# A fused attention and local-attention kernel: first loads reordered and halved, seven warm-up matmuls for ten, and the last result block handled in two halves of its rows

## The chip, the cores and the metric

The kernel runs on one core of a Trainium2 chip. The metric is the device time in microseconds of one execution. A core has five engines with instruction streams of their own: PE (TensorE: matmuls, with PEld for its weight loads), DVE (VectorE), ACT (ScalarE), POOL (GpSimd) and SP (SyncE). Engines wait for each other, and for transfers, through semaphores. SP and ACT also issue transfers between memory and the core. Such an issue takes time in the issuing engine's own stream, and whatever stands behind it in that stream waits until it is done.

## What is computed

The input x has 4 images of 64 x 64 pixels and 256 channels, in float32. Two layers follow each other:

```
# layer 0, over all 4096 pixels of an image
q = x @ Wq + bq ; k = x @ Wk + bk ; v = x @ Wv + bv        # 32, 32, 256 channels
x = gamma * softmax(q k^T) v + x
# layer 1
perceived = depthwise 3x3 convolution of x, 3 outputs per channel, + b_perc
dx = W_up2 gelu(W_up1 perceived + b_up1) + b_up2
h = x + dx
out = h + local attention of h over each pixel's 3x3 window
```

## The kernel before

Channels lie on the 128 partitions, in two halves c = 0 and c = 1 (`CH` = 2). An image's pixels are cut into 8 blocks ("slots") of 512 pixels, that is 8 rows of 64; there are 32 slots in all. For each slot the main loop (line 1088) runs through 16 points. At each it forms energies (line 304), their exponentials (line 312) and the product with the values (line 323), while the convolution, the two-step update and the local attention of slots two to five places back are put in between. The order of the work on each engine is the order of the program's text (`manual_schedule`, line 1614).

**The start.** `renew(slot, cs)` (line 123) issues on SP's queue a load of one slot's rows of x into a ring tile `xp`; slots 0 and 1 come as one transfer for each channel half, slots 2 and 3 as one each. On ACT's queue go the weights `wqk` (line 129) and `wv` (line 131, through `loaded`, line 79), and then four small transfers that put the bias `bqk` on four groups of 32 partitions (line 138). While these run, PE executes `WARM` = 10 matmuls of a tile of ones with itself (line 152); a float32 matmul shows as two passes in the trace, so the trace has 20 of them. `fetch(0)` and `fetch(1)` (line 202) copy the arrived rows into dense tiles `xc`: half c = 0 by DVE (line 227), half c = 1 by ACT (line 229). ACT's first such instruction is preceded by an `ACT_TABLE_LOAD` that the compiler puts there; the trace shows it under line 229.

The first matmuls of the computation are those of `project_v(0, 0)` (line 263): for each of two groups of 128 pixels, the product with `wv[:, 0, :]` and then that with `wv[:, 1, :]`:

```
for i in range(2):
    for kin in range(CH):
        nc.tensor.matmul(ps[:, i * C : (i + 1) * C],
            lhsT=xc[:, kin, bass.ts(2 * pair + i, P)], rhs=wv[:, kin, :], ...)
```

So the second matmul needs half c = 1 of `xc` and of `wv`. Next come `project_qk(0)` (line 231; it needs `wqk` and both halves of slots 0 and 1) and the other products of `wv`. ACT drains these (lines 242 and 275), and SP and ACT send the keys and queries on to other partitions (lines 246, 254, 259) before the energies of slot 0 can begin.

**The end.** After the last slot of the main loop, the last blocks are finished one after another (lines 1219 to 1249). The last is slot 31: `local_product(last, 0)` (line 1259) and `local_product(last, 1, judge)` (line 1266), one for each channel half. Each is a group of matmuls (line 1025), a DVE multiplication with the reciprocal sums (line 1042), a DVE addition of the residual (line 1050) and a store on SP's queue (line 1051). `behind` is given only in the second of these two calls: `judge` (line 1261) sums a check of all values over the partitions and writes the flag `bad`. Every engine then reads that flag (`TENSOR_LOAD`, line 1616) and jumps over a second version of the whole computation (`COMPARE_BRANCH`, line 1616), which isn't executed here. Behind the jump the engines meet (line 1661), SP after it has waited for all transfers, and the program ends.

## Time and profile before

Four executions took 3455.48 to 3456.39 us, with a median of 3455.88 us.

| | |
|---|---|
| the profiled execution's own time | 3456.07 us |
| its span, from the first instruction to the last | 3454.2 us |
| granted TensorE clock over the span | 0.999 |
| instructions | 33708 |
| idle time of PE before the first matmul of the warm-up | 1.07 us |
| PE busy between 0 and 120 us | 117.2 us |
| last DVE instruction of the computation ends | 3449.47 us |

The transfers of the start, in the order of their issue on each queue:

| queue | what | issued at, us | KB | issue to landing, us |
|---|---|---|---|---|
| ACT | wqk | 0.8 | 64 | 3.2 |
| SP | x, slot 0, c = 0 | 0.8 | 264 | 3.0 |
| ACT | wv | 1.3 | 256 | 4.0 |
| SP | x, slot 0, c = 1 | 1.3 | 264 | 3.8 |
| SP | x, slot 1, c = 0 | 1.7 | 264 | 4.3 |
| ACT | bqk, first three | 1.7, 2.2, 2.7 | 0.1 | 4.5, 4.2, 4.0 |
| ACT | bqk, fourth | 3.9 | 0.1 | 3.0 |
| SP | x, slot 1, c = 1 | 4.0 | 264 | 3.0 |
| SP | x, slot 2 | 5.3 | 528 | 4.3 |
| SP | x, slot 3 | 6.0 | 528 | 4.9 |

And the two stores of the last slot, both on SP's queue: the first is issued at 3448.1 us and has landed 2.0 us later, the second is issued at 3449.5 us and has landed 2.9 us later; 256 KB each.

In lines of the profile, an engine's name with a q (SPq, ACTq) is its instruction stream: issues of transfers, waits, branches. In the chain of waits the columns are start, duration and what ran; in the rows of a timeline they are start, duration, engine, line, operation and count; in the view of one source line the numbers behind "x1:" are the shortest, median and longest duration in ns, and then the start of the first and last in us.

### The profile page before, as it was taken

The page shows a single profiled execution, that of the slowest core. Times are in us where ns is not written, and L with a number is a line of the kernel's source. Part 1 is how long each engine was busy: PE and PEld are TensorE (multiplying, and loading weights), DVE is VectorE, ACT ScalarE, POOL GpSimd, SP SyncE. Part 2 cuts the span into 40 slices and gives each one's busy share as a digit, 9 for nine tenths or more (in the row PEclk, how much of TensorE's full clock was granted, in tenths as well). Part 3 has the DMA queues.
Part 4 walks back from the last instruction along what each step waited for, and adds up shares of the span by engine and source line. Part 5 has one row for each costly group of instructions (what it writes and reads, how often), then busy time and mean ns, then how long its engine had stood idle before and what let it go on. Part 6 is the DMA issues. An engine that isn't in the chain of part 4 may idle for free.

```text
span 3454.2 us, 33708 instructions
## 1 busy us (share of the span) xinstructions
PE 3441.8 (100%) x12726; PEld 1999.5 (58%) x12726; DVE 2738.8 (79%) x4439; ACT 1064.0 (31%) x1328; POOL 359.5 (10%) x525
## 2 busy tenths in 40 slices
PE   9999999999999999999999999999999999999999
PEld 5445555556555556566555555566656555555555
DVE  2388888767888888876888888887688888888895
ACT  3232333323332233332333323333233333223331
POOL 2000001110111110111001111101110111110021
PEclk9999999999999999999999999999999999999999
DMA  3000000120000000012000000001100000000000
GB/s 107 7 4 10 7 10 16 28 47 18 16 13 10 16 16 16 22 25 46 16 10 16 10 13 16 16 22 30 42 16 16 16 10 7 16 16 18 7 7 26
DMA packets 93274, 67.05 MB, mean 19 GB/s; under 512 B 65872, under 2 KB 71248, under 8 KB 92976
## 3 DMA queue, kind: packets, MB, share of 16 engines
q1 hardware_dynamic: 92432, 64.42, 6.8%
q8 instruction: 102, 1.67, 0.2%
q14 instruction: 68, 0.56, 0.1%
q10 hardware_dynamic: 672, 0.39, 0.0%
HBM read 43.62 MB, written 18.81 MB: 18 GB/s over the span
## 4 chain that ended last, share of the span: by engine, by line
PE 98%; DVE 1%; SPq 0%; DMA 0%; ACT 0%; issue 0%; ACTq 0%; POOL 0%; DVEq 0%
PE acc L323 51%; PE e L304 8%; PE hid_gf L582 4%; PE hid_de L582 4%; PE hid_bc L582 4%; PE lv L891 3%; PE v L270 3%; PE lo L1025 3%; PE s L932 3%; PE hid_a L582 3%; PE dx_ab L534 2%; PE dx_eg L534 1%; PE dx_cd L534 1%; PE hid L614 1%; PE g_cd L534 1%; PE qk L236 1%
## 5 line engine op out<-in xcount | busy, mean ns | idle before, releaser
L323 PE MATMUL acc<-p,v 128*128 128x512 f32 x4096 | 1835.2, 594 | 0.3 <-DVE o L388 0.3
L323 PEld LDWEIGHTS acc<-p,v 128*128 128x128 f32 x4096 | 770.0, 190 | 808.0 <-issue 791.4
L477 DVE SCALAR_TENSOR_TENSOR perc<-xp,wperc,perc 128x512 f32<-128x512 f32 (+2 forms) x1554 | 1103.0, 772 | 27.5 <-ACT perc L473 27.4
L312 ACT ACTIVATE p<-e 128x1024 f32<-128x1024 f32 x512 | 524.0, 1024 | 1717.8 <-PE e L304 713.2
L337 DVE TENSOR_TENSOR den<-den,p 128x1024 f32<-128x1024 f32 x480 | 587.4, 1224 | 86.4 <-ACT p L312 84.7
L957 POOL TENSOR_TENSOR lp<-lp,near 128x396 f32<-128x396 f32 x60 | 97.0, 1617 | 2490.7 <-ACT lp L952 2490.7
L304 PE MATMUL e<-qa,ka 32*128 32x512 f32 x2048 | 292.1, 640 | 0.0
L304 PEld LDWEIGHTS e<-qa,ka 32*128 32x128 f32 x2048 | 80.1, 183 | 166.0 <-issue 145.1
L582 PE MATMUL hid_de<-perc,wmix 128*128 128x256 f32 x720 | 165.2, 379 | 0.0
L582 PEld LDWEIGHTS hid_de<-perc,wmix 128*128 128x128 f32 x720 | 137.1, 190 | 43.4 <-issue 21.5
L483 DVE TENSOR_TENSOR perc<-perc 128x256 f32<-128x256 f32 x360 | 153.6, 441 | 8.2
L605 ACT ACTIVATE hid<-hid,bup 128x512 f32<-128x512 f32 x120 | 80.1, 714 | 219.5 <-DVE hid L589 219.5
L473 ACT ACTIVATE perc<-xp,bperc,wperc 128x512 f32<-128x512 f32 x192 | 145.3, 805 | 1.8 <-DVE xp L394 1.8
L980 POOL TENSOR_TENSOR lsum<-lsum,lp 128x99 f32<-128x99 f32 x168 | 122.3, 734 | 11.0
L1025 PEld LDWEIGHTS lo<-lp,lv 128*128 128x128 f32 x732 | 102.9, 191 | 35.0 <-issue 27.2
L891 PE MATMUL lv<-wlv,h 128*128 128x256 f32 x520 | 122.4, 380 | 0.0
L589 DVE TENSOR_TENSOR hid<-hid_bc,hid 128x512 f32<-128x512 f32 x60 | 41.5, 692 | 101.7 <-PE hid_bc L582 101.7
L270 PE MATMUL v<-wv,xc 128*128 128x256 f32 x512 | 116.6, 380 | 0.1
L270 PEld LDWEIGHTS v<-wv,xc 128*128 128x128 f32 x512 | 97.1, 190 | 28.0 <-issue 14.8
L932 PEld LDWEIGHTS s<-lq,h 128*128 128x128 f32 x520 | 87.1, 188 | 37.3 <-issue 27.4
L891 PEld LDWEIGHTS lv<-wlv,h 128*128 128x128 f32 x520 | 99.0, 191 | 15.3 <-issue 2.1
L1025 PE MATMUL lo<-lp,lv 128*128 128x99 f32 (+1 forms) x732 | 107.5, 296 | 0.0
(194 smaller groups left out, 3108.6 us busy)
## 6 DMA issues: line engine op xcount, KB each, us to landing
xp<-in_x SPq DMA_DIRECT2D x30, 528.0 KB, 4.0
xc<-in_x SPq DMA_DIRECT2D x56, 256.0 KB, 3.6
out<-lo SPq DMA_DIRECT2D x56, 256.0 KB, 2.0
qa<-packed SPq DMA_DIRECT2D x124, 64.0 KB, 2.0
out<-res SPq DMA_DIRECT2D x8, 256.0 KB, 2.0
ka<-st SPq DMA_DIRECT2D x124, 16.0 KB, 1.8
packed<-st SPq DMA_DIRECT2D x31, 64.0 KB, 1.9
wup<-in_w_up SPq DMA_DIRECT2D x1, 1536.0 KB, 6.8
```

The costliest lines, as they stand in the source:

```text
L270: nc.tensor.matmul(ps[:, i * C : (i + 1) * C], lhsT=xc[:, kin, bass.ts(2 * pair + i, P)], rhs=wv[:, kin, :], start=(kin == 0), stop=(kin = ...
L304: nc.tensor.matmul(e[:, j, :], lhsT=key[rows, :], rhs=queries[s][rows, :], start=True, stop=True,)
L312: nc.scalar.activation(p, energies[s, G][:, 2 * half : 2 * half + 2, :], AF.Exp)
L323: nc.tensor.matmul(accs[s][c], lhsT=v[:, 2 * half + i, bass.ts(c, P)], rhs=p[:, i, :], start=(first and i == 0), stop=(G == NG - 1 and hal ...
L337: nc.vector.tensor_tensor(den, den, p, ALU.add)
L477: nc.vector.scalar_tensor_tensor(acc, win, wt, acc, ALU.mult, ALU.add)
L483: nc.vector.tensor_tensor(t[:, to, :], t[:, a, :], t[:, b, :], op)
L534: nc.tensor.matmul(ps[:, n * C : (n + 1) * C], lhsT=w(j), rhs=values(j), start=(j == 0), stop=(j == kin - 1),)
L582: nc.tensor.matmul(ps[:, n * C : (n + 1) * C], lhsT=w(j), rhs=mixes[s, j][:, kind, :], start=(j == 0), stop=(j == MULT - 1),)
L891: nc.tensor.matmul(ps[:, half * C : (half + 1) * C], lhsT=keys_of(s, t, half, kin), rhs=wlv[:, kin, :], start=(kin == 0), stop=(kin == CH ...
L932: nc.tensor.matmul(ps[:, t * QR * QW : t * QR * QW + rows * QW].rearrange("p (h w) -> p h w", w=QW), lhsT=keys_of(s, t, half, kin), rhs=gu ...
L1025: nc.tensor.matmul(pv[:, rows, columns(half)], lhsT=lvs[block, t, half][:, bass.ts(c, P)], rhs=near_ws[block, half][:, t, of, :], start=(i ...
```

## The change

`WARM` goes from 10 to 7. On ACT's queue `wv` comes first, as two transfers of one half each, and `wqk` after them; `wv` has the same tile as before, so `loaded` is no longer used for it. The loads on SP's queue keep their order. In `local_product`, the call that is given `behind`, which is that of slot 31 and c = 1 alone, does the residual and the store in two halves of four rows: each half has an addition of its own, and the first half's store goes out on SP's queue, the second's on ACT's. `KR` is 4 and n * C is n * 256 pixels, which is four rows.

```
-WARM = 10
+WARM = 7
...
         wqk = pool.tile([P, CH, 2, CQK], F32, tag="wqk", name="wqk")
+        wv = const.tile([P, CH, C], F32, tag="wv", name="wv")
+        nc.scalar.dma_start(out=wv[:, 0, :], in_=w_v[:, 0, :])
+        renew(0, slice(0, 1))
+        nc.scalar.dma_start(out=wv[:, 1, :], in_=w_v[:, 1, :])
+        renew(0, slice(1, 2))
         nc.scalar.dma_start(out=wqk, in_=w_qk)
-        renew(0, slice(0, 1))
-        wv = loaded(w_v, "wv", queue=nc.scalar)
-        renew(0, slice(1, 2))
         renew(1, slice(0, 1))
         renew(1, slice(1, 2))
...
             ov, rv = (t.rearrange("p (h a w) -> p h a w", a=2, w=KW) for t in (o, res))
-            nc.vector.tensor_tensor(rv, ov, pixels(s, c), ALU.add)
-            nc.sync.dma_start(out=out[b, :, c, bass.ts(g, NB)], in_=res)
+            if not behind:
+                nc.vector.tensor_tensor(rv, ov, pixels(s, c), ALU.add)
+                nc.sync.dma_start(out=out[b, :, c, bass.ts(g, NB)], in_=res)
+                return
+
+            for n, queue in enumerate((nc.sync, nc.scalar)):
+                rows = slice(n * KR, (n + 1) * KR)
+                nc.vector.tensor_tensor(rv[:, rows], ov[:, rows], pixels(s, c)[:, rows], ALU.add)
+                at = g * NB + n * C
+                queue.dma_start(out=out[b, :, c, at : at + C], in_=res[:, bass.ts(n, C)])
```

## The prediction

> **What bounds it now.** I read the page first: busy time of the engines and the chain of work that ended last.

> ```profile
> PE 3441.8 (100%) x12726; PEld 1999.5 (58%) x12726; DVE 2738.8 (79%) x4439; ACT 1064.0 (31%) x1328; POOL 359.5 (10%) x525
> ...
> PE 98%; DVE 1%; SPq 0%; DMA 0%; ACT 0%; issue 0%; ACTq 0%; POOL 0%; DVEq 0%
> ```

> PE is busy throughout, so what an edit away from PE can be worth lies before PE runs without gaps and behind its last matmul: some 6 us at the front and 7 us at the back. Both edits lie there. The second view is the chain of waits over the first 16 us:

> ```profile
> 0.82 3.03 DMA xp<-in_x
> 3.84 0.02 issue
> 3.86 0.32 ACTq L138
> 4.18 0.03 issue
> 4.21 1.28 ACT L229
> 5.49 0.01 issue
> 5.50 0.63 ACT xc L229
> 6.13 0.04 issue
> 6.18 1.56 PE v L270 x6
> ```

> The start hangs on ACT, not on the warm-up: the fourth bias transfer (L138) is issued only when the first half of x has landed at 3.84; behind it stand the table load and the copy of half c = 1, and PE's second product (the third of its eight passes) starts at 6.18. From that landing to PE it is 6.18 - 3.84 = 2.34 us. Why should a bias transfer wait for x? The waits of SP's queue tell, with the time of two landings (the transfers issued at 1.3 and 1.7):

> ```profile
> SPq L126 <- DMA wqk<-in_w_qk: 1.8, 1, 1.8
> SPq L126 <- DMA wv<-in_w_v: 1.0, 1, 1.0
> ```

> ```profile
> DMA to landing us min/median/max: 3.8/4.0/4.3
> ```

> Eight transfers go out without a wait: wqk, x0c0, wv, x0c1, bqk, x1c0, bqk, bqk. The ninth (x1c1) waits for wqk, the first; the tenth (fourth bqk) for x0c0, the second; the eleventh (x, slot 2) for wv, the third. So each transfer waits for the one eight places before it. x0c1, the fourth, lands at 1.27 + 3.8 = 5.06.

> Third, the row of the warm-up against later matmuls, in the timeline:

> ```profile
> 1.07 4.44 PE L152 MATMUL warm<-ones 128*128 128x128 f32 x20 [1.07 <-POOL ones L144]
> 9.54 5.45 PE L270 MATMUL v<-wv,xc 128*128 128x256 f32 x24
> ```

> A pass over 128 columns takes 4.44 / 20 = 0.22 us, later one over 256 columns 5.45 / 24 = 0.23: the array runs at half rate until about 5.2 us (the last of the warm-up's weight loads, at 5.1, is down from 334 to 244 ns), 4.1 us after its first pass.

> Last, the view of line 1616 for the end:

> ```profile
> L1616 ACTq COMPARE_BRANCH  x1: 54/54/54, 3448.7 to 3448.7; - x1
> ...
> L1616 DVEq COMPARE_BRANCH  x1: 72/72/72, 3449.7 to 3449.7; - x1
> ...
> L1616 SPq COMPARE_BRANCH  x1: 50/50/50, 3450.5 to 3450.5; - x1
> ...
> L1616 ACTq EVENT_SEMAPHORE  x1: 17/17/17, 3451.8 to 3451.8; - x1
> L1616 PEldq EVENT_SEMAPHORE  x1: 51/51/51, 3452.4 to 3452.4; - x1
> L1616 DVEq EVENT_SEMAPHORE  x1: 21/21/21, 3453.2 to 3453.2; - x1
> ```

> From branch to next instruction ACT needs 3.1 us and DVE 3.5. DVE, whose branch stands behind the last addition, comes last at 3453.2; the last store has landed at 3449.5 + 2.9 = 3452.4. So the end is set by a branch, not by the store, and the span closes 1.0 us behind it.

> **The change, part by part.** *Warm-up.* Three matmuls fewer are 6 passes of 0.213 us, 1.28 us of PE. The warm-up isn't in the chain: it ends at 5.5, the second product waits for ACT until 6.18. The two passes that can run earlier (about 4.4, when wv's first half and DVE's copy, 3.86 + 0.43, are there) hide in the same wait. Worth 0.

> *Order and halves of the loads.* wv in two halves makes thirteen transfers of twelve and seven issues on ACT of six. Before, the two queues took their places as A S A S A S A A S A S S; kept up, the new list is wv0, x0c0, wv1, x0c1, wqk, x1c0, bqk, bqk, x1c1, bqk, x slot 2, bqk, x slot 3. The third bqk is tenth and waits for x0c0 (about 3.9); the fourth is twelfth and waits for x0c1, the fourth: 5.06 instead of 3.84. Behind it on ACT stand the table load and the copy, and PE waits for these: 5.06 + 2.34 = 7.40 instead of 6.18, +1.22 us. Bounds: if no ACT issue had to wait, seven of 0.47 (0.81, 1.26, 1.74) would end at 4.1, the table load at 5.4, and PE would start at 6.07, -0.1. If the wait is for wv1 and this lands as late as the whole wv (1.3 + 4.0 = 5.3), +1.46. I take 1.22, since the places of the two queues are read from this trace. Transfers that move otherwise have cover: x1c1 now waits for wv0 (as wqk 3.2 to as wv 4.0 after 0.81, so 4.0 to 4.8), lands 3.0 later at 7.8 at most and is copied in 0.62, while its use, the second half of qk, moves to 7.40 + 1.56 + 0.93 = 9.9; without the shift it could cost 0.4. wqk, third on ACT at 1.74, lands by 6.2 at the first bqk's 4.5, ahead of qk at 9.0. The slot 2 load waits for wv1 instead of wv, no later than before.

> The shift goes on undiminished: behind 6.18 the chain is PE's v and qk, ACT's drains and issues, SP's issues, each started by the one before it; PE then is busy for good.

> *The clock.* Fourteen passes end at about 4.3, the two early products at half rate (0.43 each) at 5.3; then PE is idle until 7.40. If the full rate still comes at 5.2, this costs 0. If the 4.1 us start anew at 7.40, it comes at 11.5 and (11.5 - 7.4) / 2 = 2.05 us are lost. The four executions already differ by 0.9, about what a rate change moved by 1.8 us would do; I take half of that, 0.4, near the lower end since the array is all but gapless from 1.07 to 5.3.

> [...]

> *The end.* Additions over 128x256 take 0.42 each, two in a row 0.76 (L904), against 0.69 now (L1050): DVE's last is +0.07. SP's store goes out 0.3 us earlier, hidden since stores don't end last. ACT's own store is new: its stream now stands at the second half until 3449.54, issues, reads the flag and branches. SP did just that from 3449.5 and branched at 3450.5; so ACT at 3450.6 instead of 3448.7, and at its 3.1 us it is back at 3453.7, behind DVE's 3453.2: +0.5. Bounds: as quick as SP's own branch (SP goes on at 3450.7), and DVE decides: +0.1; PE's 3.6 (3448.8 to 3452.4): +1.0. I take ACT's own row. ACT's store lands by 3449.6 + 2.9 = 3452.5 and stays hidden.

> **Sum.** 1.22 + 0.4 + 0.5 = +2.1 us. The profiled execution took 3456.07 (span 3454.2, 1.9 around it): 3458.2. It lies 0.19 above the median 3455.88, so 3458.0 is the forecast. A difference under 0.2% (6.9 us) is about what a measurement of this kernel can't tell from no change; the forecast is +0.06%.

> **Rivals.** *The full rate comes late* (slower). Place: the matmuls from 7.40 on; price: half of the time from there to the full rate, on top of 1.7 us. At 11.5 it gives 3459.7, at 14 it gives 3460.9. It makes the kernel slower by more than 6.9 us from the point where the rate changes at 17.8 or later, which needs 10 us of half rate. For it: the gap from 5.3 to 7.4. Against: after 7.4 PE has work without such gaps, so a third try of 4.1 us is unlikely.

> *ACT isn't held* (the places of the queues differ, or the fourth bqk waits for x0c0): PE starts at 6.07 to 6.6, and the end alone remains: 3455.88 + 0.5 = 3456.4. For it: the places are inferred. Against: seven ACT transfers can't all be among the first eight unless SP's loads are held instead.

> *The halves pay* (faster): the first product's earlier start and a quicker last store show fully; at best -0.1 at the front, the clock always in time (the spread's half, -0.4), end 0: 3455.4. Against: both ends are set by ACT and by branches, which get more work. Over 6.9 us faster isn't to be had here: the front until 6.18 and the branches remain.

> **How the numbers follow.** Forecast 0.50 (own range 3456.8 to 3459.0), late rate 0.25, ACT not held 0.13, halves pay 0.12. Lowest -0.1 - 0.4 + 0.1 = -0.4, less half the spread of runs, 0.45: 3455.0. Highest 1.46 + 2.05 + 1.0 = 4.5, plus 0.45: 3460.9. Within 6.9 us: 0.93; slower beyond it: 0.05 (a fifth of the late-rate case); faster beyond it: 0.02 for what I don't see.

> **What would show it.** In the chain of waits: the fourth L138 behind x0c1 at 5.06, the table load at 5.4, PE's v going on at 7.4. In the timeline: passes of v over 256 columns at 0.43 behind 7.4 would mean a late rate. At line 1616: ACT's branch at 2 us later relative to DVE's and ACT the last to come back. I am wrong if ACT's table load starts before 4.5, or DVE still comes last.

## The result, and the profile after

The changed kernel takes 3459.52 us in the median (40 runs, 3457.69 to 3460.48); beside them the kernel before took 3455.73 us (60 runs, 3455.25 to 3456.39). The ratio is 1.0011 with an interval of 1.0006 to 1.0015, so it is 3.8 us, or 0.11%, slower. That is below the 0.2% taken in the prediction as the limit of a measurement; with this many runs the interval still leaves out 1.

The profiled execution took 3459.95 us. The first rows of the page show the same bound as before:

```profile
span 3457.9 us, 33701 instructions
...
PE 3443.5 (100%) x12720; PEld 1995.0 (58%) x12720; DVE 2738.5 (79%) x4440; ACT 1064.4 (31%) x1328; POOL 360.6 (10%) x525
```

Against before the span grew by 3.8 us (3454.18 to 3457.95 when not rounded) and PE's busy time by 1.7, although PE executes six passes less. So there are longer waits and slower passes. Both are in the timeline of PE over the first 40 us (start, duration, engine, line, operation, count):

```profile
1.07 3.35 PE L154 MATMUL warm<-ones 128*128 128x128 f32 x14 [1.07 <-POOL ones L146]
5.42 1.22 PE L272 MATMUL v<-wv,xc 128*128 128x256 f32 x2 [1.00 <-DVE xc L229]
8.39 2.93 PE L272 MATMUL v<-wv,xc 128*128 128x256 f32 x6 [1.75 <-ACT xc L231]
11.25 2.83 PE L238 MATMUL qk<-xc,wqk 128*64 128x512 f32 x8
14.01 5.45 PE L272 MATMUL v<-wv,xc 128*128 128x256 f32 x24
...
36.09 1.98 PE L238 MATMUL qk<-xc,wqk 128*64 128x512 f32 x6 [0.40 <-DMA xc<-in_x]
```

The same rows before:

```profile
5.43 2.31 PE L270 MATMUL v<-wv,xc 128*128 128x256 f32 x8
7.67 1.94 PE L236 MATMUL qk<-xc,wqk 128*64 128x512 f32 x8
...
32.05 1.93 PE L236 MATMUL qk<-xc,wqk 128*64 128x512 f32 x6 [0.84 <-DMA xc<-in_x]
```

The third pass of v starts at 8.39 (before: 6.18). Six passes of v take 2.93 us (before: 1.56) and eight of qk 2.83 (before: 1.94 from 7.67 on), so the array runs at half rate until about 13. The trace's record of the grant of the full clock stands at 13.09 (before: 5.18). The 24 passes of v start at 14.01 instead of 9.54, that is 4.47 us late.

The timeline of ACT tells why PE waits until 8.39:

```profile
2.22 4.18 ACTq L140 DMA_DIRECT2D bqk<-in_b_qk  x4
6.43 1.28 ACT L231 ACT_TABLE_LOAD   x1 [6.43 <-DMA wv<-in_w_v]
7.72 1.14 ACT L231 COPY xc<-xp 128x512 f32<-128x512 f32 x2
```

The four bias issues hold ACT until 6.40, and what ends the wait is a half of `wv`. It landed at 6.06, and the fourth bias transfer is issued at 6.08. SP's queue waits in the same way, each issue for the transfer eight places before it: the second half of slot 1 is issued at 5.1 (the first half of `wv` has landed at 5.09), slot 2 at 5.89 (the second half of slot 0, 5.88) and slot 3 at 7.0 (`wqk`, 6.9). Its view (waited for, then us in total, times, longest):

```profile
SPq L126 <- DMA wv<-in_w_v: 2.9, 1, 2.9
...
SPq L126 <- DMA xp<-in_x: 0.4, 1, 0.4
SPq L126 <- DMA wqk<-in_w_qk: 0.4, 1, 0.4
```

Landings after (before in brackets): first half of slot 0 at 4.91 (3.84), second half at 5.88 (5.06), the halves of `wv` at 5.09 and 6.06 (the whole at 5.30).

At the end, the view of line 1626, which is where the branch now stands:

```profile
L1626 DVEq COMPARE_BRANCH  x1: 72/72/72, 3453.4 to 3453.4; - x1
...
L1626 ACTq COMPARE_BRANCH  x1: 58/58/58, 3454.2 to 3454.2; - x1
...
L1626 PEldq EVENT_SEMAPHORE  x1: 51/51/51, 3456.3 to 3456.3; - x1
L1626 DVEq EVENT_SEMAPHORE  x1: 21/21/21, 3456.6 to 3456.6; - x1
L1626 ACTq EVENT_SEMAPHORE  x1: 17/17/17, 3457.1 to 3457.1; - x1
```

ACT branches 0.8 us behind DVE (before: 1.0 ahead of it) and is the last to come back, as forecast. Yet from the last multiplication's start to the end of the span it is 6.20 us, against 6.12 before.

### The profile page after: what moved, and what is told of

Read it like the earlier page. It is cut to its first block, busy times and chain, and to the rows that moved or that the text cites. A ratio compares the mean times of both kernels' runs of the same rounds, so it can differ in the third digit from the quotient of the medians.

```text
span 3457.9 us, 33701 instructions
## 1 busy us (share of the span) xinstructions
PE 3443.5 (100%) x12720; PEld 1995.0 (58%) x12720; DVE 2738.5 (79%) x4440; ACT 1064.4 (31%) x1328; POOL 360.6 (10%) x525
## 4 chain that ended last, share of the span: by engine, by line
## 5 line engine op out<-in xcount | busy, mean ns | idle before, releaser
L959 POOL TENSOR_TENSOR lp<-lp,near 128x396 f32<-128x396 f32 x60 | 97.0, 1616 | 2490.6 <-ACT lp L954 2490.6
```

## The experiments

The theory after this reading has four parts. ACT's hold delays PE by some 2 us. The shorter warm-up makes the full rate come late, which costs some 2 us more. A little is given back later. The end costs next to nothing. The rival puts all of it on the hold, or on the new loads as such. Each kernel ran 11 times on the chip beside the kernel before (33 runs for each of three sets). "Difference" is between those medians. Most intervals of the ratios are about 0.09% (3 us) to each side, so a single difference below that is not certain by itself. The reading rests on the profiles and on how the differences fit together.

### Set 1: the warm-up and the end, alone (before: 3455.76 us)

The changed kernel with the old warm-up:

```
-WARM = 7
+WARM = 10
```

> The changed kernel with ten warm-up matmuls instead of seven; loads and end as changed. Theory: two causes at the start. ACT is held, so that the second product of v starts at about 8.4 us, and the idle gap before it keeps the array at half rate until about 13 us. Ten matmuls fill PE until about 6.4 instead of 4.4, so the gap shrinks from 3 us (with one short piece of work in it) to 2 us, and the full rate should come earlier in most executions: 3458.5 us (3457.5 to 3459.3), second product still at 8.4. Rival, the late loads alone and no part of the array's rate: 3459.5, as the changed kernel. Rival, the shorter warm-up alone: 3455.8, as before.

Measured: 3457.28 us, difference +1.52, ratio 1.0006 (0.9997 to 1.0015), a little below the expected 3457.5 to 3459.3. Seven executions lie at 3457.1 to 3457.4 and four at 3458.9 to 3459.4. The profiled one is of the upper four. These are its windows between the records of the granted clock (window, length, busy time of PE, PEld, DVE, ACT and POOL, then PEclk, DMA share, GB/s; PEclk reads 1.00 ahead of the first record too, where the passes go at half rate: 15 begin in 3.19 us, 0.21 each for 128 columns, and later 24 of 256 columns take 5.45, 0.23 each):

```profile
0.85:4.26 3.41, 3.19 (x15) 3.19 (x16) 0.12 (x1) 0.00 (x0) 3.09 (x15) 1.00 0.68 176
4.26:7.67 3.41, 1.33 (x9) 0.92 (x8) 1.05 (x2) 1.67 (x2) 3.03 (x11) 1.00 0.89 262
7.67:11.08 3.41, 3.12 (x8) 2.10 (x10) 0.47 (x1) 0.91 (x3) 2.98 (x13) 0.50 0.85 288
```

The full rate was granted at 4.26, withdrawn at 7.67, and granted again at 11.08. Between them PE was busy for 1.33 of 3.41 us, because it waited for ACT. So ten warm-up matmuls bring the rate in time, but the hold lets it be lost in this execution. The two groups of times, 1.6 us apart, fit a rate that was kept in seven executions and lost in four. Only the upper one has a profile.

More than twice as many:

```
-WARM = 7
+WARM = 24
```

> The changed kernel with 24 warm-up matmuls, which fill PE until about 8.3 us. Theory: the second product still waits for ACT until about 8.4 us, but runs at full rate (passes over 256 columns 0.216 us apart, not 0.43), so that of the 3.8 us only the hold of 2.2 is left, less some 0.6 given back at the loads of slots 4 to 7: 3457.3 us (3456.8 to 3457.9), and the spread over the executions falls from 2.8 to about 1 us. Rival, the rate has no part: 3459.5. Rival, the shorter warm-up is all: 3455.8 or more, since the warm-up would now end later than before.

Measured: 3459.91 us (3457.50 to 3461.91), difference +4.15, ratio 1.0012 (1.0003 to 1.0021). This was a miss: at the front the profile shows what was wanted, and the time is still no better. The rate is granted at 5.63, the 24 passes of v start at 12.38 instead of 14.01, and then the gain is lost behind 18 us. This is the view of the first store of packed keys, with the wait of ACT for it:

```profile
L261 SPq DMA_DIRECT2D packed<-st x1: 578/578/578, 18.3 to 18.3; - x1
...
  ACT st L244: 3.8, 1
...
DMA to landing us min/median/max: 4.0/4.0/4.0
```

In e1 the same store lands after 1.9 us, and ACT waits 1.6 us for PE instead. The trace tells its landing in sixteen shares: here fifteen had landed by 20.18, and the last came at 22.32. In between, from 19.68, a fetch of 16 KB of instructions took 1.57 us, and the last two packets of 2 KB go out at 21.23 and 21.45, when it ends. That it shared a way with the late share fits these times, but the kept trace doesn't show it. In e1 the first such fetch starts at 23.02; e2 has 14 matmuls more, and there it comes earlier. With ACT, SP's issues come late, so that a load of later slots is issued at 31.45 (after the change: 31.49) and PE waits for it until 36.10 (36.09), and the gain is gone. One profile shows it. That it is what lengthens the median is inferred.

The kernel before with the new warm-up alone:

```
-WARM = 10
+WARM = 7
```

> The kernel before with seven warm-up matmuls and nothing else changed. Theory: the second product starts at 6.2 us as before, PE is idle from 4.4 to about 5.4 (the whole wv lands at 5.3), and the full rate comes later than at 5.2 in many executions: 3456.7 us (3456.0 to 3457.9). Rival, the rate has no part and the warm-up was cover only: 3455.7. Rival, the shorter warm-up is all of the 3.8 us: 3459.5.

Measured: 3457.20 us (3455.51 to 3457.72), difference +1.44, ratio 1.0004 (0.9995 to 1.0013). Four executions at 3455.5 to 3456.2 and seven at 3456.8 to 3457.7; before has nothing above 3456.04 in this set. The profile caught the fastest execution: granted at 4.11, span 3453.6, nothing lost. So fourteen passes can be enough. The seven slower times fit a late rate, but no trace shows one of them.

The kernel before with the new end alone:

```
-            nc.vector.tensor_tensor(rv, ov, pixels(s, c), ALU.add)
-            nc.sync.dma_start(out=out[b, :, c, bass.ts(g, NB)], in_=res)
+            if not behind:
...
+            for n, queue in enumerate((nc.sync, nc.scalar)):
...
```

> The kernel before with only the end changed: the last residual and store by halves, the second half stored from ACT's queue. Theory from the two profiles: ACT becomes the last engine to come back from the branch, 0.1 to 0.3 us behind what DVE was: 3455.9 us (3455.7 to 3456.1). As the prediction put it, +0.5: 3456.2. Rival, the earlier half store pays: 3455.4 or less.

Measured: 3455.86 us, difference +0.10, ratio 1.0001 (0.9991 to 1.0010). The view of its branch line:

```profile
L1624 DVEq EVENT_SEMAPHORE  x1: 21/21/21, 3452.2 to 3452.2; - x1
L1624 ACTq EVENT_SEMAPHORE  x1: 17/17/17, 3452.7 to 3452.7; - x1
```

ACT comes back last here too, and from the last multiplication's start to the end it is 6.25 us (before: 6.12). The new end is worth +0.1, as far as these runs tell.

### Set 2: who holds ACT (before: 3456.26 us)

The changed kernel with the bias transfers on SP's queue (e5); then also with ten warm-up matmuls and the old end, so that of the change only order and halves of the loads are left (e6); and the kernel before with its bias transfers on SP's queue (e7). The edit in all three:

```
         for r in range(4):
-            nc.scalar.dma_start(
+            nc.sync.dma_start(
                 out=bqk2[r * CQK : (r + 1) * CQK, :], in_=b_qk[:, r % 2 : r % 2 + 1]
             )
```

And in e6 besides:

```
-WARM = 7
+WARM = 10
...
-            if not behind:
...
-                queue.dma_start(out=out[b, :, c, at : at + C], in_=res[:, bass.ts(n, C)])
+            nc.vector.tensor_tensor(rv, ov, pixels(s, c), ALU.add)
+            nc.sync.dma_start(out=out[b, :, c, bass.ts(g, NB)], in_=res)
```

> The changed kernel with the four bias transfers issued on SP's queue, ahead of the loads of slots 2 and 3, instead of on ACT's; seven warm-up matmuls and the new end stay. Theory: nothing holds ACT any more, its table load starts at 2.2 us and its first copy as soon as the second half of x has landed (5.3 to 5.9), so that the second product starts at 6.0 to 6.6 instead of 8.0 to 8.4; the gap in PE shrinks and the full rate comes in time more often: 3457.0 us (3456.2 to 3458.0). Rival, the hold is no cause, and the later landing of the halved loads is: 3459.0 or more. Rival, the clock alone: 3459.0 as well, since PE's gap from 4.4 to 5.4 stays.

> The changed order and halves of the loads, with the four bias transfers on SP's queue, ten warm-up matmuls and the old end. Theory: neither hold nor gap is left, the second product starts at 6.0 to 6.3 as before, at full rate as often as before: 3455.8 us (3455.3 to 3456.5). Rival, the halved loads cost by themselves: 3457.3, what the changed kernel with ten warm-up matmuls took.

> The kernel before with the four bias transfers on SP's queue, ahead of the loads of slots 2 and 3, and nothing else. Theory: ACT's table load starts at 1.8 instead of 4.2 us, its copy at the landing of the second half of x, 5.1 instead of 5.5, and the second product at 5.8 instead of 6.2: 3455.4 us (3455.0 to 3455.7). Rival, the table load was no part of what bounded the start: 3455.8. Rival, the loads of slots 2 and 3 behind four more issues come late: 3456.3 or more.

Measured: e5 3457.65 us, difference +1.39, ratio 1.0004 (0.9995 to 1.0013); e6 3455.79, −0.47, 0.9998 (0.9989 to 1.0007); e7 3455.32 (3454.87 to 3456.25), −0.94, 0.9998 (0.9989 to 1.0007). The timeline of ACT in e5, then that of PE:

```profile
2.23 1.28 ACT L231 ACT_TABLE_LOAD   x1 [2.23 <-issue]
5.38 0.62 ACT L231 COPY xc<-xp 128x512 f32<-128x512 f32 x1 [1.88 <-DMA xp<-in_x]
```

```profile
4.95 4.03 PE L272 MATMUL v<-wv,xc 128*128 128x256 f32 x8 [0.52 <-DVE xc L229]
```

The table load starts at 2.23 instead of 6.43, the copy waits for its data alone, and the third pass starts at 6.06. The hold is gone, and what is left is the rate: eight passes take 4.03 us, and the grant comes at 9.50 (this execution, 3456.95 us, is the second fastest of the eleven). In e6, with three matmuls more in the warm-up, it comes at 3.98, and nothing of the loss against before remains. In e7 the third pass starts at 6.04, hardly earlier than before's 6.18, since now PE waits for `wv`, which lands at 5.4. PE's rows in e6, then in e7:

```profile
5.68 0.70 PE L272 MATMUL v<-wv,xc 128*128 128x256 f32 x2 [0.74 <-DVE xc L229]
6.76 1.56 PE L272 MATMUL v<-wv,xc 128*128 128x256 f32 x6 [0.38 <-ACT xc L231]
```

```profile
5.53 1.97 PE L270 MATMUL v<-wv,xc 128*128 128x256 f32 x8 [0.36 <-DMA wv<-in_w_v]
```

e6 and e7 differ by the order and halves of the loads alone: e6 is 0.47 us slower in the median, and its third pass starts at 6.76 instead of 6.04, since the first half of x lands at 5.08 instead of 3.97. So wv ahead of wqk, in halves, may cost about half a microsecond by itself, which so few runs can't tell from nothing. What it cost above that came through the place that it gave the fourth bias transfer.

A warm-up that lasts until the data come, without more instructions (e8: the changed kernel with ten matmuls over 256 columns):

```
-WARM = 7
+WARM = 10
...
-nc.tensor.matmul(warm[:, :P], lhsT=ones, rhs=ones, ...)
+nc.tensor.matmul(warm[:, :C], lhsT=ones, rhs=watched[:, :C], ...)
```

> The changed kernel with ten warm-up matmuls of 256 columns instead of 128, so that PE stays busy until about 7.6 us with the instructions of the run with ten narrow ones. Theory: the rate doesn't fall back before the second product starts at about 8.0, the passes of v are 0.216 us apart: 3457.2 us (3456.8 to 3457.7), without the upper group that four of the eleven times with ten narrow ones fell into (3458.9 to 3459.4). Rival, that group has another cause than the rate: it stays. If the slow time with 24 matmuls (3459.9) came from the code of the longer warm-up, whose fetch delayed a store that ACT waits for, it doesn't come back here; if it came from the longer warm-up itself, it does.

Measured: 3458.40 us (3457.86 to 3459.37), difference +2.14, ratio 1.0007 (0.9998 to 1.0016). The time lies above the expected 3457.7; the eleven are spread over 1.5 us without a group of their own at the top. The grant comes at 5.22 and stays, and the 24 passes start at 11.59. In e2 they start 0.8 us later, since its warm-up lasts until 8.85 and so past ACT's copies: that much of e2's loss is the warm-up's length. The store of packed keys lands in 1.9 us here, which speaks for the instructions as the cause of the rest.

### Set 3: order, repeats (before: 3456.11 us)

The changed kernel with wqk first again, wv's halves behind it (e9); the changed kernel itself on the same chip (e10); e8 again (e11); e7 again (e12). The edit of e9:

```
+        nc.scalar.dma_start(out=wqk, in_=w_qk)
         nc.scalar.dma_start(out=wv[:, 0, :], in_=w_v[:, 0, :])
...
-        nc.scalar.dma_start(out=wqk, in_=w_qk)
```

> The changed kernel with wqk issued ahead of the two halves of wv on ACT's queue; seven warm-up matmuls and the new end stay. Theory: what runs beside the first load of x decides when it lands; beside the small wqk it lands at 3.8 to 4.0 us as before, not at 4.2 to 5.1; the fourth bias transfer waits for the first half of wv (about 4.8) and the second product starts at about 7.1 instead of 8.0 to 8.4. The rate mostly still comes late, so about 0.8 us less than the changed kernel on the same chip. Rival, the first load lands late whatever runs beside it because there are more transfers: 4.2 or later, and no time is gained.

> The changed kernel itself, beside the other three on the same chip, for a second profile. Theory: 3.8 us over the kernel before on this chip (3.3 to 4.3); second product at 8.0 to 8.4, full rate between 8 and 13.1 us. If its first profile was a rare one, the second product starts before 7.6.

> The changed kernel with ten wide warm-up matmuls again, now beside the changed kernel itself: the hold and the later landing stay, the late rate is gone. Theory: 2.1 us over the kernel before on this chip, so 1.7 us less than the changed kernel, which is the part of the rate. Rival, the rate has no part: the same time as the changed kernel.

> The kernel before with the bias transfers on SP's queue, again, on another set of runs: if its gain of 0.9 us is real, 0.4 to 1.0 us less than the kernel before on this chip; if it was chance, within 0.2 of it.

Measured: e9 3459.92 us, difference +3.81, ratio 1.0011 (1.0002 to 1.0020); e10 3460.22, +4.11, 1.0012 (1.0003 to 1.0021); e11 3458.18, +2.07, 1.0006 (0.9997 to 1.0015); e12 3455.69 (3455.11 to 3456.20), −0.42, 0.9998 (0.9989 to 1.0007).

PE's timeline in e10, then in e11:

```profile
8.04 2.93 PE L272 MATMUL v<-wv,xc 128*128 128x256 f32 x6 [1.92 <-DMA bqk<-in_b_qk]
10.89 2.98 PE L238 MATMUL qk<-xc,wqk 128*64 128x512 f32 x8
13.80 5.45 PE L272 MATMUL v<-wv,xc 128*128 128x256 f32 x24
```

```profile
8.11 1.56 PE L272 MATMUL v<-wv,xc 128*128 128x256 f32 x6 [0.27 <-ACT xc L231]
9.60 1.94 PE L238 MATMUL qk<-xc,wqk 128*64 128x512 f32 x8
11.47 5.45 PE L272 MATMUL v<-wv,xc 128*128 128x256 f32 x24
```

Third pass of v at the same time within 0.1 us, and then 5.76 us against 3.36 until the 24 passes: the rate alone is worth 2.4 us there and 2.04 us in the medians. The remaining 2.07 us of e11 are the hold and the end.

In e9 ACT's table load starts at 5.47 and the third pass at 7.43, 0.6 earlier than in e10, because the fourth bias transfer here waits for the first half of `wv`, which is now the third transfer and lands at 5.10 (in e10 it waits for the second half, 5.66). But the grant comes at 12.77, so the passes ahead of it run at half rate (six of v take 2.93 us in both), and of the 0.61 us at the third pass 0.43 are left at the 24 passes (13.37 against 13.80). The median is 0.3 us less instead of the expected 0.8, within what the two sets of runs scatter.

Put together, as differences to before: hold and short warm-up +4.11 (e10), hold and long warm-up +2.07 (e11), no hold and short warm-up +1.39 (e5), neither, with the old end, −0.47 (e6); e5 and e6 are from set 2. If the two causes added up, the fourth would be 2.07 + 1.39 − 4.11 = −0.65 with the new end; with the old one −0.75. The two do add up, within 0.3 us, as far as medians of eleven tell.

The kernel before with its bias transfers on SP (e7, e12) is the best version found, −0.94 and −0.42 us. Both sets agree in sign, but neither interval leaves out 1, so a gain of half a microsecond to one is likely and not certain. e12's profile doesn't show it at the start: there the grant comes at 6.75 and the 24 passes start at 9.86, against 5.18 and 9.54 before.

## Why the prediction was right in the main, and where its sum was wrong

The forecast was 3458.0 us with 3455.0 to 3460.9 about it; the time is 3459.5. The sign, the place and both mechanisms of the front were forecast. The total of +3.8 lies outside the forecast's own range (3459.0) and at the price of the first rival, the late full rate (3459.7). That the rival is so near is partly luck, since its parts are off in both directions. By steps, in the profiled executions:

| step | forecast, us | profile, us | other evidence |
|---|---|---|---|
| ACT's hold: third pass of v | +1.22 | +2.21 (e10: +1.86) | e5: gone with the bias on SP |
| the clock: third pass to the 24 passes of v | +0.4 (at most 2.05) | +2.26 | e10 less e11: 2.04 |
| given back later | 0 | −0.8 | traces only |
| the end | +0.5 | +0.1 | e4: +0.1 |
| span | +2.1 | +3.8 | medians: +3.8 |

**The hold.** Mechanism right, size too small by 1.0 us. The step "the fourth is twelfth and waits for x0c1, the fourth: 5.06 instead of 3.84" took landings from the trace of before. From the landing that ended the wait to PE it was 2.33 us, as forecast (2.34); the landing itself came 1.0 later than the 5.06 put in. In the changed kernel all the first loads land later: the first half of x at 4.91 and not at 3.84, the second at 5.88 and not at 5.06. The wait was not even for that one but for the second half of wv (6.06), the third transfer: the fourth bias transfer and the load of slot 2 had changed places, and the latter, forecast as "no later than before", was issued at 5.89 instead of 5.32. "+1.46 if the wait is for wv1" was the named bound, and it fell too, since its 5.3 was also an old landing.

**The clock.** This is the term that was mis-sized most. "Worth 0" for three matmuls fewer, and 0.4 us "near the lower end since the array is all but gapless from 1.07 to 5.3" were wrong. The array is not gapless: it stands from 4.42 to 5.42, since the first half of x lands late, and then from 6.64 to 8.39. The warm-up's work wasn't in the chain, but in e6 the full rate is granted at 3.98 while the ten matmuls still run (until 4.94), and with seven it came at 13.09 after the change. That a longer warm-up makes the difference is read from e10 against e11 (2.04 us). In e3, with the old loads, seven of eleven executions were still 1.1 to 2.0 us over before's median; that this was the rate is inferred. Nor does the full rate come a fixed 4.1 us after PE begins, as both cases of the forecast took it: with the same ten matmuls begun at 1.07 it was granted at 3.98 in e6, 4.26 in e1, 5.18 before and 6.75 in e12. The records of e1 stand 3.41 us apart; the table at the end shows how busy PE was in stretches of that length.

**"The shift goes on undiminished"** failed by 0.8 us. At 36 us the load of later slots is waited for 0.40 us, where before 0.84 were lost at the same place: the load was issued 4.18 us later (31.49 for 27.31) and landed 4.03 later, while PE was 4.47 late. The second product of qk is 4.47 us late; by 88 us PE is 3.86 late, and 3.68 at the last multiplication. Of the 0.8, the two timelines show 0.44 at that wait and 0.23 in the next group of qk, where eight passes take 2.82 us (before: 3.05) instead of the 1.94 without a wait. The rest is open, and no experiment tried it.

**The end.** ACT comes last out of the branch, as forecast, but it returns after 2.9 us and not 3.1, and the span then closes 0.9 behind it instead of 1.0 behind DVE. The size is that of the lower bound, +0.1, though not its reason, which was DVE as the last. The 3.1 was one execution's row: in the five profiles with the old end ACT returns after 2.7 to 3.1 us, in the nine with the new one after 2.8 to 3.0.

**Cover.** The halves and their order were costed at nothing beside the hold. Against before e6 agrees (−0.47); against e7 it is 0.47 slower, which so few runs can't tell from nothing.

**The rivals.** "ACT isn't held" and "the halves pay" are out by the first profile. The late rate is what came on top of the hold; its argument against, that PE has no such gaps behind 7.4, was beside the point: the gap from 6.64 to 8.39 lies ahead of the passes that ran at half rate until 13.09, while with PE busy from 1.33 to 7.82 (e8) the grant came at 5.22 and stayed.

Open: e1's lower seven executions lie 1.4 to 1.6 us above before, e11 2.07. Where this half microsecond comes from wasn't settled.

## What to carry to other kernels

A warm-up that isn't on the chain of waits may still be worth its length (here 2.04 us, e10 less e11): before shortening it, ask how long PE will stand ahead of the first real matmuls, with the landings of the new order. Here it stood for 1.00 and 1.75 us, and the full rate came at 13.09 instead of 5.18. Before a transfer is added to or moved on the queue of an engine that also computes, count which earlier transfer each issue will wait for (here the one eight places before: the fourth bias transfer went out at 6.08, when the second half of wv had landed at 6.06). The four small transfers cost less on SP's queue, whose engine does no computing here: ACT's table load then starts at 2.23 instead of 6.43 (e5). And landings shift with what is issued beside them, so a sum at the start of a kernel made with old landings can come out too low, as the one here by 1.0 us.

## What the runs showed of the hardware

**How busy PE was before the rate changed.** The records of e1 stand 3.41 us apart. For windows of that length that end at a record, or lie a whole number of them away from one, these are PE's busy time and what followed. That the rate goes by such windows in the other kernels too is the author's estimate from e1 alone:

| kernel, window, us | busy, us | rate after it |
|---|---|---|
| before, 1.77 to 5.18 | 3.41 | granted |
| e1, 0.85 to 4.26 | 3.19 | granted |
| e1, 7.67 to 11.08 | 3.12 | granted again |
| e3, 0.70 to 4.11 | 3.04 | granted |
| e6, 0.57 to 3.98 | 2.91 | granted |
| e5, 2.68 to 6.09 | 2.89 | stays at half |
| e10, 2.79 to 6.20 | 2.85 | stays at half |
| after, 2.85 to 6.26 | 2.41 | stays at half |
| e3, 4.11 to 7.52 | 2.27 | full rate kept |
| e1, 4.26 to 7.67 | 1.33 | full rate lost |

**The first load depends on its neighbour.** The first half of x lands at 3.81 to 3.97 in the six profiles where the 64 KB of wqk are issued beside it, and at 4.24 to 5.08 in the eight where 128 KB of wv are. In e9 it took 3.1 us from issue to landing, after the change 4.1 (in e10 3.6).

**A store beside a fetch of instructions.** In e2 one share of a store landed 2.1 us after the other fifteen while a fetch of 16 KB ran, and ACT's wait was 3.8 us instead of 1.6; the connection is read from the times of one profile. PE's passes of qk and of the energies around the fetch take 1.94 and 1.14 us, as in e1.

**The way out of the branch.** From the branch to the next instruction it takes 2.9 us on ACT, 3.2 on DVE, 3.8 on PE after the change; before, 3.1, 3.5 and 3.6.
